# Chunk middles in column groups, the context's keys and values a stage earlier, and softmax sums inverted pair by pair, in a four-layer decoder

## The chip, the cores and the metric

The kernel runs on one core of a Trainium2 chip. The number that counts is the device time of one execution in microseconds (us). Here PE is the matrix engine, PEld its weight loads, DVE the vector engine, ACT the scalar engine, POOL GpSimd and SP the engine that issues most loads.

## The reference, cut to what matters

A decoder of four layers works on 8 batches of 56 tokens with 256 channels, in float32. Each layer is attention, cross attention and a feed-forward part, each added to x and followed by a layer norm. The change bears on three of the twelve stages: layer 1's attention (32 heads of 8, over all keys, quantized in chunks), layer 1's cross attention (16 heads of 16, causal, keys and values from the context, of which the causal mask leaves the first 56 rows) and layer 2's attention (16 query heads of 16, causal).

```python
def _chunk_decompose(x2d):                      # chunks of 32 tokens
    ch_bias = (jnp.max(xp, axis=1, keepdims=True) + jnp.min(xp, axis=1, keepdims=True)) / 2
    xz = xp - ch_bias
    ...
    result = _sym_qdq(xz, scale[:, None, :])
    return (result, ch_bias, T)

def proj(w_orig, w_dq_t, b):
    y = result @ w_dq_t + ch_bias @ w_orig.T
    return y.reshape(-1, H)[:n] + b
...
probs = jax.nn.softmax(attn, axis=-1)
ctx = jnp.einsum('bhqk,bkhd->bqhd', probs, V).reshape(bsz * tgt, H)
r2, cb2, n2 = _chunk_decompose(ctx)
out = (r2 @ WO + cb2 @ o_weight.T).reshape(-1, H)[:n2] + o_bias

x = _layernorm(x + _L1_attn_ref(x, ...))
x = _layernorm(x + _L1_xattn_ref(x, ctx_512, ...))
```

So each projection of layer 1's attention is a product of the quantized remainder, plus a product of the chunk middles (14 chunks of 32 of the 448 tokens) that is the same for the 32 tokens of a chunk, plus a bias.

## The kernel before

Tokens lie in 4 tiles of 112 (two batches each), channels in 2 halves of 128. A scheduler orders each engine's instructions by their dependences; `mm(..., fixed=True)`, `ordered` and `keep_in_program_order` pin those that it must leave where the program has them. Weights of a stage are loaded by SP during the stage before. On-chip sums (PSUM) have eight banks: in these stages two double banks (`bank2`), two single ones (`bank`) and the pair `ps_o`. A float32 product is run by PE in two passes, each its own row of the trace.

**l1_attn** (line 1527). `decompose` (L1485) takes on DVE the maxima and minima of chunks, the middles `mid` (128×28: 14 chunks by 2 channel halves), and the quantized remainder `res`. `middles` (L1556) multiplies `mid` by the undequantized weights: for each of q, k, v in turn two products of 128 rows with 14 weight columns and one of 1 row for the bias, into 14 rows of `ps_gb`; ACT copies these into `gb`, 128 rows of which POOL has zeroed (L1559). Its products are pinned. Then keys and queries `ps_q` (L368, two halves each): two products with `res` and a third with `sel`, a table of 128 rows of which 14 aren't zero and which repeats a chunk's middle over its 32 tokens. `head_values` (L1326) does the same for the values, per batch and per parity of heads, in 64-column groups (`ps_v`, L1340), and copies them into `VX`, zeroed by POOL first (L1332): ACT the even heads, DVE the odd ones. `head_keys` (L1361) spreads keys over heads into `KX`, first half of the batches on DVE, second on POOL (L1370).

`small_heads` (L1379) runs over units (a tile and, with heads of 8, a channel half: 8 units; 4 with heads of 16): scores `ps_s` (PE), their maxima `mx` (DVE L1415), the difference `E` (DVE L1418), the exponential (ACT L1419), sums over keys (DVE L1420), transposes `ps_eT` (PE, ACT copies), and the outputs `ps_o` (PE) of the unit before. After all units one reciprocal of 128×128 sums (L1461), one transpose `ps_rec` (L1463), four DVE products with a block table into `recT` (L1467), then `ps_den`, which spreads the inverted sums over channels, and the product with `num` (L1472).

A second `decompose` of the outputs, `middles` of the output weight and `finish` (L425) follow: per tile `ps_y` (two products with `res2`, one with `sel`), added to X on DVE (L450), moments, then `norm` (L455): DVE L417, ACT's square root (L418), DVE L419 to L422, the normalized X (L459); then PE transposes X to `xT`, ACT copies it (L471).

**l1_xattn** (line 1604). Its k (`ps_k`) is a product of the context (64 rows) and is made after xT is started; KX, VX as above; q (`ps_q`) from `xT`; then `small_heads` and `finish`. **l2_attn** (line 1633) differs in q and k only, and calls the same helpers.

Of the kernel before, what the change touches and what calls it, by code (L numbers as in the profile page):

```python
# [144 lines left out]
def _pack(i):  # L145
# [40 lines left out]
    w["l1a_b"] = np.concatenate([i[p + n + "_bias"] for n in "qkvo"])[None, :]  # L186
    w["l1a_s"] = _beside(_spread(8), (np.arange(T)[None, :] // 32 == np.arange(T // 32)[:, None]).astype(np.float32))

# [76 lines left out]
class Decoder:  # L265
# [1059 lines left out]

    def head_values(self, pool, terms, dk, groups=16):  # L1326

# [5 lines left out]
        for g in range(NB // per):  # L1333
# [10 lines left out]
            for odd in range(2):  # L1344
                rows = slice(odd * 64, odd * 64 + S)
                copy = nc.vector.tensor_copy if odd else nc.scalar.copy
                to, of = VX[rows, g * per : (g + 1) * per], ps[rows, : per * n]
                if dk == 8:
                    to = to.rearrange("p b (x y) n -> p (b x) y n", y=2)
                    of = of.rearrange("p (z y n) -> p z y n", y=2, n=8)  # L1350
                    for y in range(2):
                        at = 16 * y + 8 * odd
                        copy(to[:, :, y, at : at + 8], of[:, :, y, :])
                else:
                    same = 16 // groups
                    to = to.rearrange("p b (x y) n -> p (b x) y n", y=same)[:, :, :, 16 * odd : 16 * odd + 16]
                    of = of.rearrange("p (z n) -> p z n", n=16).unsqueeze(2).to_broadcast([S, per * groups // 2, same, 16])
                    copy(to, of)
        return VX

    def head_keys(self, pool, k, dk):  # L1361

# [3 lines left out]
        for half in range(2):  # L1366
            bs = slice(half * NB // 2, (half + 1) * NB // 2)
            for c in range(2):
                of = k[:, c, :].rearrange("p (b s) -> p b s", s=S)[:, bs].unsqueeze(2).to_broadcast([128, NB // 2, n, S])
                (nc.gpsimd if half else nc.vector).tensor_tensor(KX[:, c, bs], of, hm, ALU.mult)  # L1370
        return KX
# [7 lines left out]
    def small_heads(self, pool, q, KX, VX, dk, causal, scale, spread, oT):  # L1379
# [54 lines left out]
        def outputs(n):  # L1434
            t, unit = units[n]
            eT = ets.pop(n)
            for u in range(2):
                b = 2 * t + u
                for j in range(8):
# [10 lines left out]
                    )  # L1450

        scores(0)
        for n in range(len(units)):
# [3 lines left out]
            if n:  # L1457
                outputs(n - 1)
        outputs(len(units) - 1)
        rec = sums.rearrange("p t i -> p (t i)")  # L1460
        nc.vector.reciprocal(rec, rec)  # L1461
        ps = self.bank("ps_rec")
        nc.tensor.transpose(ps[:, :128], rec, ident)  # L1463
        recT = pool.tile([128, NT, 2, S], F32, bufs=1, name="recT")
        of = ps[:, :128].rearrange("p (u q) -> p u q", u=2)[:, :, :S]
        for t in range(NT):
            nc.vector.tensor_scalar_mul(recT[:, t], of, self.const("blocks")[:, t : t + 1])  # L1467
        nc.scalar.copy(num, acc[:, :, :T])
        for c in range(2):
            ps = self.bank("ps_den")  # L1470
            self.mm(ps[:, :T], [(spread[:, c * 128 : (c + 1) * 128], recT.rearrange("p t u q -> p (t u q)"))])
            nc.vector.tensor_tensor(oT[:, c, :], ps[:, :T], num[:, c, :], ALU.mult)  # L1472
# [54 lines left out]
    def l1_attn(self):  # L1527
# [5 lines left out]
        (bias,) = self.parts("l1a_b")  # L1533
        spread, sel = self.fields("l1a_s", D, T)
        with tc.tile_pool(name="l1a", bufs=2) as pool:
            dT = pool.tile([128, 4, 2, D], F32, bufs=1, name="dT")
# [18 lines left out]

            def middles(mid, first, n):  # L1556

                out = pool.tile([128, n, D], F32, bufs=1, name="gb")
                nc.gpsimd.memset(out, 0.0)  # L1559
                ps = self.bank2("ps_gb")  # L1560
                for j in range(n):
                    self.mm(
                        ps[:G, j // 2, j % 2 * D : (j % 2 + 1) * D],
                        [(mid[:, c * G : (c + 1) * G], wT(first + j, c)) for c in range(2)]
                        + [(self.ones[:1, :G], bias[:, (first + j) * D : (first + j + 1) * D])],
                        fixed=True,
                    )
                for j in range(0, n, 2):
                    m = min(2, n - j)
                    nc.scalar.copy(out[:G, j : j + m, :].rearrange("p j n -> p (j n)"), ps[:G, j // 2, : m * D])  # L1570
                return out

            mid = self.decompose(pool, self.xT, res)
            gb = middles(mid, 0, 3)
            q, k = self.head_queries(pool), pool.tile([128, 2, T], F32, bufs=1, name="k")
            for m in (1, 0):
                ps = self.bank2("ps_q1")
                for o in range(2):
                    at = slice(o * 128, (o + 1) * 128)
                    self.mm(ps[:, o, :T], [(dT[:, m, c, at], res[:, c, :]) for c in range(2)] + [(gb[:, m, at], sel)])  # L1580
                    if m:
# [5 lines left out]
            def value_terms(b, odd):  # L1587
                at = slice(b * S, (b + 1) * S)
                own = lambda a: a.rearrange("p (x y n) -> p x y n", y=2, n=8)[:, :, odd, :]
                return [(res[:, c, at], own(dT[:, 2, c, :])) for c in range(2)] + [(sel[:, at], own(gb[:, 2, :]))]  # L1590

            VX = self.head_values(pool, value_terms, 8, 32)
            oT = pool.tile([128, 2, T], F32, bufs=1, name="oT1")
            self.small_heads(pool, q, KX, VX, 8, False, 8.0**-0.5, spread, oT)
            res2 = pool.tile([128, 2, T], F32, bufs=1, tag="res", name="res2")
            mid = self.decompose(pool, oT, res2)
            gb2 = middles(mid, 3, 1)
            self.finish(
                early=False,
                terms_of=lambda t: [(res2[:, c, self.tok(t)], dT[:, 3, c, :]) for c in range(2)] + [(sel[:, self.tok(t)], gb2[:, 0, :])]  # L1600
            )


    def l1_xattn(self):
        nc, tc, xT = self.nc, self.tc, self.xT
        wq, wo = self.fields("l1x_1", 512, 512)
        wk, wv, cT = self.fields("l1x_2", D, D, T)
        wq, wo = (a.rearrange("p (c n) -> p c n", c=2) for a in (wq, wo))
        (spread,) = self.fields("l1x_t", D)
        with tc.tile_pool(name="l1x", bufs=2) as pool:  # L1610
            q = self.head_queries(pool)
            k = pool.tile([128, 2, T], F32, bufs=1, name="k")
            qps, kps = self.bank2("ps_q"), self.bank2("ps_k")
            for o in range(2):
                self.mm(kps[:, o, :T], [(wk[:DC, o * 128 : (o + 1) * 128], cT[:DC, :])])
            nc.scalar.copy(k, kps[:, :, :T])
            KX = self.head_keys(pool, k, 16)

            def value_terms(b, odd):
                own = wv[:DC, :].rearrange("p (x y n) -> p x y n", y=2, n=16)[:, :, odd, :]  # L1620
                return [(cT[:DC, b * S : (b + 1) * S], own)]

            VX = self.head_values(pool, value_terms, 16)
            for o in range(2):
# [274 lines left out]
```

## Time and profile before

| | us |
|---|---|
| median of 3 runs (lowest to highest) | 1665.28 (1662.88 to 1666.53) |
| profiled execution | 1665.35 |
| its span in the trace | 1663.1 |

The trace's windows give the stages around the change (busy us of each engine, and the granted clock of PE as a share of full speed):

| window | length | PE | DVE | ACT | POOL | clock |
|---|---|---|---|---|---|---|
| 494 to 569: norm, decompose, projections and heads of l1_attn | 75 | 58.64 | 52.19 | 25.37 | 15.54 | 0.82 |
| 569 to 605: second decompose, l1_attn's finish, start of l1_xattn | 36 | 22.40 | 22.38 | 5.12 | 5.26 | 0.67 |
| 605 to 634: heads and finish of l1_xattn | 29 | 21.34 | 20.70 | 11.59 | 3.52 | 0.94 |
| 735 to 782: l2_attn | 47 | 37.71 | 29.74 | 13.74 | 11.56 | 0.96 |

These 187 us are a ninth of the span. The granted clock of the whole execution is 0.926, so the first two windows run at a lower clock than the rest. In the trace's lines a product is written with its weight's shape (rows×columns of weights), the shape of the moving operand, and the number of passes; times are the start in us from the beginning of the span, and the length.

### The profile page before, as it was taken

What the parts mean: (1) busy time and instruction counts of PE and PEld (TensorE: products, weight loads), DVE (VectorE), ACT (ScalarE), POOL (GpSimd) and SP (SyncE); (2) the same over time, 40 slices, a digit from 0 to 9 for tenths busy, and PEclk for the clock granted to TensorE, in tenths of its full rate; (3) what the DMA queues carried; (4) which work ended last, traced back from release to release, by engine and by line L of the source; (5) the groups of instructions that cost most, each with busy time, mean ns of one, the idle gap of its engine ahead of it and who ended that gap; (6) DMA issues with size and microseconds to landing.
All of it is one profiled execution on the core that took longest, in us unless ns stands there. A gap on an engine that the chain in (4) does not pass through costs nothing.

```text
span 1663.1 us, 37875 instructions
## 1 busy us (share of the span) xinstructions
PE 1499.5 (90%) x16428; PEld 894.4 (54%) x16428; DVE 1095.2 (66%) x1793; ACT 625.2 (38%) x915; POOL 323.9 (19%) x302
## 2 busy tenths in 40 slices
PE   7989989999788678998989999899987978999898
PEld 4666435556644344565435555655555834555656
DVE  0575579999475855326569999635474239999633
ACT  2431245655312422103245556332343144566320
POOL 4711511212123010011521122101131000221200
PEclk9999979999897878999988999999997987999989
DMA  9523422323020001222332322121220361323100
GB/s 359 188 79 108 123 56 84 96 83 88 18 87 28 26 27 35 78 70 74 114 86 62 110 78 81 41 64 55 83 64 27 119 172 38 104 72 88 41 1 11
DMA packets 52088, 133.76 MB, mean 80 GB/s; under 512 B 20673, under 2 KB 21137, under 8 KB 51922
## 3 DMA queue, kind: packets, MB, share of 16 engines
q1 hardware_dynamic: 19906, 65.36, 12.0%
q10 hardware_dynamic: 28368, 50.25, 10.8%
q0 software_dynamic: 3648, 15.73, 2.9%
q8 instruction: 129, 2.11, 0.5%
q14 instruction: 37, 0.30, 0.1%
HBM read 119.06 MB, written 6.75 MB: 76 GB/s over the span
## 4 chain that ended last, share of the span: by engine, by line
PE 49%; DVE 9%; issue 8%; ACT 2%; DMA 1%; POOL 1%; ACTq 1%; DVEq 0%; POOLq 0%
PE ps_x L376 17%; PE ps_glu L368 8%; PE ps_y L368 7%; PE ps_qk L1675 2%; DVE sc L376 2%; PE ps_v L1675 2%; PE ps_qh L368 2%; PE ps_big L368 1%; PE ps_y L1675 1%; PE ps_q L368 1%; PE ps_qk L376 1%; PE ps_m L376 1%; PE ps_s L1397 1%; DVE E L1418 1%; DVE mx L1415 1%
## 5 line engine op out<-in xcount | busy, mean ns | idle before, releaser
L376 PE MATMUL ps_x<-kvT,qa 64*128 64x375 f32 x1344 | 310.4, 567 | 29.1 <-DVE sc L376 23.1
L376 ACT ACTIVATE sc<-sc,tops 128x1500 f32<-128x1500 f32 x168 | 259.2, 1544 | 151.7 <-DVE sc L376 118.3
L376 DVE STREAM_TRANSPOSE eT<-sc 128x1536 f32<-128x1536 f32 x168 | 297.1, 1768 | 11.7 <-PE ps_x L376 9.5
L376 PE MATMUL ps_x<-eT,kv 32*64 32x224 f32 x9024 | 257.7, 357 | 3.7 <-issue 3.2
L376 PEld LDWEIGHTS ps_x<-eT,kv 32*64 32x64 f32 x9024 | 197.6, 133 | 70.1 <-issue 59.8
L376 PEld LDWEIGHTS ps_x<-kvT,qa 64*128 64x128 f32 x1344 | 114.3, 201 | 187.2 <-DVE sc L376 160.4
L376 DVE TENSOR_SCALAR_CACHE_REDUCE sc<-ps_x 128x750 f32<-128x750 f32 x168 | 157.3, 936 | 38.4 <-PE ps_x L376 38.2
L376 DVE TENSOR_SCALAR_CACHE_REDUCE sc<-ps_x,tops 128x750 f32<-128x750 f32 x168 | 161.1, 959 | 1.3 <-PE ps_x L376 1.1
L376 POOL TENSOR_TENSOR eT<-eyes,sums 128x224 f32<-128x224 f32 x24 | 13.3, 555 | 453.6 <-DVE sums L376 453.6
L827 POOL TENSOR_TENSOR rope<-rope,turn 96x448 f32<-96x448 f32 x64 | 71.0, 1130 | 65.0 <-DVE turn L825 65.0
L824 DVE TENSOR_TENSOR rope<-ps_big,consts 96x896 f32<-96x896 f32 x32 | 34.8, 1086 | 58.4 <-PE ps_big L368 58.4
L1190 ACT ACTIVATE act<-ps_glu 128x448 f32<-128x448 f32 (+1 forms) x52 | 28.3, 544 | 111.7 <-PE ps_glu L368 108.4
L1194 DVE TENSOR_TENSOR act<-ps_glu,act 128x448 f32<-128x448 f32 x43 | 26.8, 624 | 65.2 <-ACT act L1190 65.1
L418 ACT ACTIVATE rstd<-rstd 112x3 f32<-112x3 f32 (+2 forms) x21 | 4.3, 204 | 166.2 <-DVE rstd L417 166.1
L624 DVE RECIPROCAL rec<-rec 128x896 f32<-128x896 f32 x8 | 46.0, 5753 | 27.0 <-ACT rec L623 27.0
L376 PE MATMUL ps_x<-wm,qa 128*112 128x128 f32 (+1 forms) x336 | 53.5, 318 | 9.7 <-DVE qa L376 9.7
L450 DVE TENSOR_TENSOR X<-X,ps_y 112x256 f32<-112x256 f32 x32 | 13.5, 421 | 70.6 <-PE ps_y L368 70.6
L376 PEld LDWEIGHTS ps_x<-wm,qa 128*112 128x112 f32 x336 | 45.2, 191 | 21.7 <-issue 11.2
L1758 POOL TENSOR_TENSOR qk<-qk,sw 128x896 f32<-128x896 f32 x16 | 33.3, 2083 | 101.3 <-DVE sw L1757 78.8
L376 POOL TENSOR_TENSOR qa<-num,rec 64x448 f32<-64x448 f32 x42 | 47.9, 1140 | 2.9
L754 ACT COPY qa<-ps_qk 64x448 f32<-64x448 f32 x48 | 25.3, 527 | 60.0 <-PE ps_qk L376 46.1
L376 POOL DMA_DIRECT2D kvT<-kvT x24 | 13.7, 573 | 122.7 <-DVE X L450 49.2
(410 smaller groups left out, 2424.2 us busy)
## 6 DMA issues: line engine op xcount, KB each, us to landing
kv<-kv ACTq DMA_DIRECT2D x288, 128.0 KB, 2.7
kvT<-kvT POOLq DMA_DIRECT2D x24, 384.0 KB, 3.5
qa<-qa ACTq DMA_DIRECT2D x24, 224.0 KB, 3.6
raw<-in_ctx ACTq DMA_DIRECT2D x6, 512.0 KB, 4.3
kv<-raw POOLq DMA_DIRECT2D x6, 512.0 KB, 4.2
kvT<-by POOLq DMA_DIRECT2D x6, 512.0 KB, 4.3
l0a_q<-in_l0a_q SPq DMA_DIRECT2D x4, 512.0 KB, 10.6
l0a_c<-in_l0a_c SPq DMA_DIRECT2D x4, 512.0 KB, 8.8
```

What stands on the lines that cost most here:

```text
L368: ins = self.nc.tensor.matmul(out, lhsT, rhs, start=n == 0, stop=n == len(terms) - 1)
L376: call(*args, **kw)
L624: nc.vector.reciprocal(rec, rec)
L754: nc.scalar.copy(flat[rows, :, odd, h // 2 * S : (h // 2 + 1) * S], ps[rows, :T].rearrange("p (b s) -> p b s", b=NB))
L824: nc.vector.tensor_tensor(rope.rearrange("p a (b s) -> p a b s", b=NB), view, cos, ALU.mult)
L827: nc.gpsimd.tensor_tensor(rope[:, half, :], rope[:, half, :], turn[:, 1 - half, :], ALU.add)
L1190: nc.scalar.activation(act, ps[:m, 0, :T], AF.Silu)
L1194: nc.vector.tensor_tensor(act, ps[:m, 1, :T], act, ALU.mult)
L1397: tc.keep_in_program_order(nc.tensor.matmul(*args, **kw))
L1415: nc.vector.tensor_reduce(mx, view, AX.X, ALU.max)
L1675: tc.keep_in_program_order(nc.tensor.matmul(*args, **kw))
L1758: nc.gpsimd.tensor_tensor(qk, qk, sw, ALU.add)
```

## The change

- `middles` takes a list of weights. The contraction half is the outer loop and the weight the inner one; weight j gets rows 32j to 32j+13 of its own bank, so that the three go to three column groups of PE. `gb` has one column block, with weight j in rows 32j to 32j+13, copied by ACT in one copy a weight; it is no longer zeroed. The table `sel` is repeated each 32 rows, and the third term of `ps_q`, `ps_v` and `ps_y` uses 14 rows of it instead of 128.
- `small_heads` inverts the 128×32 sums of a tile as soon as its units are done, in the loop. Four transposes of 128×32 replace the one of 128×128; they put all tiles into 32 rows, so that one copy of 32×448 replaces the four products with the block table, and `ps_den` contracts 32 rows. All three stages use it.
- `l1x_context` makes l1_xattn's k and VX inside l1_attn, between `small_heads` and the second `decompose`, in a pool of its own opened ahead of l1_attn's. Both halves of the values are copied by ACT.
- `head_keys` with `alone` runs all four KX products on DVE, in program order; l1_xattn uses it.

In issue order, on PE `ps_k` and l1_xattn's `ps_v` move from behind l1_attn's finish to between `ps_den` and the second `ps_top`; on POOL that stage's VX memset moves ahead of l1_attn's KX, and its two KX products are gone. SP's loads are the same in the same order.

```diff
     w["l1a_b"] = np.concatenate([i[p + n + "_bias"] for n in "qkvo"])[None, :]
-    w["l1a_s"] = _beside(_spread(8), (np.arange(T)[None, :] // 32 == np.arange(T // 32)[:, None]).astype(np.float32))
+    w["l1a_s"] = _beside(_spread(8), (np.arange(T)[None, :] // 32 == np.arange(128)[:, None] % 32).astype(np.float32))
...
-    def head_values(self, pool, terms, dk, groups=16):
+    def head_values(self, pool, terms, dk, groups=16, copies=None):
...
                 rows = slice(odd * 64, odd * 64 + S)
-                copy = nc.vector.tensor_copy if odd else nc.scalar.copy
+                copy = (copies or (nc.scalar.copy, nc.vector.tensor_copy))[odd]
                 to, of = VX[rows, g * per : (g + 1) * per], ps[rows, : per * n]
...
-    def head_keys(self, pool, k, dk):
+    def head_keys(self, pool, k, dk, alone=False):
...
                 of = k[:, c, :].rearrange("p (b s) -> p b s", s=S)[:, bs].unsqueeze(2).to_broadcast([128, NB // 2, n, S])
-                (nc.gpsimd if half else nc.vector).tensor_tensor(KX[:, c, bs], of, hm, ALU.mult)
+                to = KX[:, c, bs]
+                if alone:
+                    self.ordered(nc.vector.tensor_tensor, to, of, hm, ALU.mult)
+                else:
+                    (nc.gpsimd if half else nc.vector).tensor_tensor(to, of, hm, ALU.mult)
         return KX
...
+        per = len(units) // NT
         scores(0)
...
                 outputs(n - 1)
+            if n % per == per - 1:
+                nc.vector.reciprocal(sums[:, n // per], sums[:, n // per])
         outputs(len(units) - 1)
-        rec = sums.rearrange("p t i -> p (t i)")
-        nc.vector.reciprocal(rec, rec)
         ps = self.bank("ps_rec")
-        nc.tensor.transpose(ps[:, :128], rec, ident)
-        recT = pool.tile([128, NT, 2, S], F32, bufs=1, name="recT")
-        of = ps[:, :128].rearrange("p (u q) -> p u q", u=2)[:, :, :S]
         for t in range(NT):
-            nc.vector.tensor_scalar_mul(recT[:, t], of, self.const("blocks")[:, t : t + 1])
+            tc.keep_in_program_order(nc.tensor.transpose(ps[:32, t * 128 : (t + 1) * 128], sums[:, t], ident))
+        recT = pool.tile([32, NT * 2, S], F32, bufs=1, name="recT")
+        nc.vector.tensor_copy(recT, ps[:32].rearrange("p (u q) -> p u q", q=64)[:, :, :S])
         nc.scalar.copy(num, acc[:, :, :T])
...
             ps = self.bank("ps_den")
-            self.mm(ps[:, :T], [(spread[:, c * 128 : (c + 1) * 128], recT.rearrange("p t u q -> p (t u q)"))])
+            self.mm(ps[:, :T], [(spread[:32, c * 128 : (c + 1) * 128], recT.rearrange("p u q -> p (u q)"))])
             nc.vector.tensor_tensor(oT[:, c, :], ps[:, :T], num[:, c, :], ALU.mult)
...
+        self.l1x = ExitStack()
+        self.l1x_pool = self.l1x.enter_context(tc.tile_pool(name="l1x", bufs=1))
         with tc.tile_pool(name="l1a", bufs=2) as pool:
...
-            def middles(mid, first, n):
-                out = pool.tile([128, n, D], F32, bufs=1, name="gb")
-                nc.gpsimd.memset(out, 0.0)
+            def middles(mid, ms):
+                out = pool.tile([128, D], F32, bufs=1, name="gb")
                 ps = self.bank2("ps_gb")
-                for j in range(n):
-                    self.mm(
-                        ps[:G, j // 2, j % 2 * D : (j % 2 + 1) * D],
-                        [(mid[:, c * G : (c + 1) * G], wT(first + j, c)) for c in range(2)]
-                        + [(self.ones[:1, :G], bias[:, (first + j) * D : (first + j + 1) * D])],
-                        fixed=True,
-                    )
-                for j in range(0, n, 2):
-                    m = min(2, n - j)
-                    nc.scalar.copy(out[:G, j : j + m, :].rearrange("p j n -> p (j n)"), ps[:G, j // 2, : m * D])
-                return out
+                banks = [ps[:, 0], ps[:, 1], self.bank("ps_gb1") if len(ms) > 2 else None]
+                for k in range(3):
+                    for j, m in enumerate(ms):
+                        of = bias[:, m * D : (m + 1) * D]
+                        lhsT, rhs = (self.ones[:1, :G], of) if k == 2 else (mid[:, k * G : (k + 1) * G], wT(m, k))
+                        self.ordered(nc.tensor.matmul, banks[j][32 * j : 32 * j + G, :D], lhsT, rhs, start=k == 0, stop=k == 2)
+                for j in range(len(ms)):
+                    nc.scalar.copy(out[32 * j : 32 * j + G], banks[j][32 * j : 32 * j + G, :D])
+                return lambda j: (out[32 * j : 32 * j + G], sel[32 * j : 32 * j + G])
             mid = self.decompose(pool, self.xT, res)
-            gb = middles(mid, 0, 3)
+            gb = middles(mid, (1, 0, 2))
             q, k = self.head_queries(pool), pool.tile([128, 2, T], F32, bufs=1, name="k")
...
                     at = slice(o * 128, (o + 1) * 128)
-                    self.mm(ps[:, o, :T], [(dT[:, m, c, at], res[:, c, :]) for c in range(2)] + [(gb[:, m, at], sel)])
+                    mine, sel_ = gb(1 - m)
+                    self.mm(ps[:, o, :T], [(dT[:, m, c, at], res[:, c, :]) for c in range(2)] + [(mine[:, at], sel_)])
                     if m:
...
                 own = lambda a: a.rearrange("p (x y n) -> p x y n", y=2, n=8)[:, :, odd, :]
-                return [(res[:, c, at], own(dT[:, 2, c, :])) for c in range(2)] + [(sel[:, at], own(gb[:, 2, :]))]
+                mine, sel_ = gb(2)
+                return [(res[:, c, at], own(dT[:, 2, c, :])) for c in range(2)] + [(sel_[:, at], own(mine))]
...
             self.small_heads(pool, q, KX, VX, 8, False, 8.0**-0.5, spread, oT)
+            self.l1x_context()
             res2 = pool.tile([128, 2, T], F32, bufs=1, tag="res", name="res2")
             mid = self.decompose(pool, oT, res2)
-            gb2 = middles(mid, 3, 1)
+            mine, sel_ = middles(mid, (3,))(0)
             self.finish(
                 early=False,
-                terms_of=lambda t: [(res2[:, c, self.tok(t)], dT[:, 3, c, :]) for c in range(2)] + [(sel[:, self.tok(t)], gb2[:, 0, :])]
+                terms_of=lambda t: [(res2[:, c, self.tok(t)], dT[:, 3, c, :]) for c in range(2)] + [(sel_[:, self.tok(t)], mine)]
             )
...
+    def l1x_context(self):
+        pool = self.l1x_pool
+        wk, wv, cT = self.fields("l1x_2", D, D, T)
+        k = pool.tile([128, 2, T], F32, name="k")
+        ps = self.bank2("ps_k")
+        for o in range(2):
+            self.mm(ps[:, o, :T], [(wk[:DC, o * 128 : (o + 1) * 128], cT[:DC, :])], fixed=True)
+        self.nc.scalar.copy(k, ps[:, :, :T])
+        def value_terms(b, odd):
+            own = wv[:DC, :].rearrange("p (x y n) -> p x y n", y=2, n=16)[:, :, odd, :]
+            return [(cT[:DC, b * S : (b + 1) * S], own)]
+        self.l1x_made = k, self.head_values(pool, value_terms, 16, copies=(self.nc.scalar.copy,) * 2)
...
         wq, wo = self.fields("l1x_1", 512, 512)
-        wk, wv, cT = self.fields("l1x_2", D, D, T)
         wq, wo = (a.rearrange("p (c n) -> p c n", c=2) for a in (wq, wo))
         (spread,) = self.fields("l1x_t", D)
-        with tc.tile_pool(name="l1x", bufs=2) as pool:
+        with self.l1x, tc.tile_pool(name="l1q", bufs=2) as pool:
+            k, VX = self.l1x_made
             q = self.head_queries(pool)
-            k = pool.tile([128, 2, T], F32, bufs=1, name="k")
-            qps, kps = self.bank2("ps_q"), self.bank2("ps_k")
-            for o in range(2):
-                self.mm(kps[:, o, :T], [(wk[:DC, o * 128 : (o + 1) * 128], cT[:DC, :])])
-            nc.scalar.copy(k, kps[:, :, :T])
-            KX = self.head_keys(pool, k, 16)
-            def value_terms(b, odd):
-                own = wv[:DC, :].rearrange("p (x y n) -> p x y n", y=2, n=16)[:, :, odd, :]
-                return [(cT[:DC, b * S : (b + 1) * S], own)]
-            VX = self.head_values(pool, value_terms, 16)
+            KX = self.head_keys(pool, k, 16, alone=True)
+            qps = self.bank2("ps_q")
             for o in range(2):
```

## The prediction

> **What bounds the kernel.** The page first. PE is busy for nine tenths of the span, and the row of granted clock falls below 9 at the stage borders; a change beside PE pays only where PE waits.
>
> ```profile
> span 1663.1 us, 37875 instructions
> PE 1499.5 (90%) x16428; PEld 894.4 (54%) x16428; DVE 1095.2 (66%) x1793; ACT 625.2 (38%) x915; POOL 323.9 (19%) x302
> ```
>
> Then the chain of waits over l1_attn, l1_xattn and l2_attn, which hold all of the edits (columns: start, length, work that carried the chain):
>
> ```profile
> 508.94 8.32 PE ps_gb L368 x18
> 517.26 9.69 PE ps_q L368 x18
> ...
> 530.20 4.94 PE ps_v L1340 x86
> 535.14 1.66 PE ps_s L1397 x16
> ...
> 581.66 8.35 PE ps_y L368 x24
> ...
> 597.82 3.35 PE ps_k L368 x4
> 601.17 3.30 PE ps_q L368 x4
> ```
>
> From 508.9 to 535.1 PE never rests: middles (ps_gb), keys and queries (ps_q), values (ps_v). ps_y is l1_attn's output, ps_k the context's keys. Then the PE windows of 3.41 us on whose borders the granted clock changes here (columns: window, length, PE busy and instructions, clock):
>
> ```profile
> 38.03:41.44 3.41, 3.41 (x32) 1.00 0.44 168
> 41.44:44.85 3.41, 3.41 (x25) 0.50 0.00 0
> ...
> 509.06:512.47 3.41, 3.41 (x8) 0.50 0.00 0
> 512.47:515.89 3.42, 3.42 (x9) 0.50 0.35 101
> ...
> 519.30:522.71 3.41, 3.41 (x6) 0.50 0.00 0
> 522.71:526.13 3.42, 3.42 (x11) 1.00 0.00 0
> ```
>
> PE is wholly busy from 509.06, but at half clock until 522.71. And the full window at 38.03, spent on products that use 8 weight rows, is followed by half clock. Windows full of 128-row products lift the clock; windows full of thin ones don't.
>
> **The change, part by part** (minus is faster; profiled execution 1665.35 us, span 1663.1; the median shown, 1665.28, is the same within 0.1).
>
> A. First norm, ahead of decompose. The chain has DVE's normalization (L459) from 498.85 for 2.26, though its tiles elsewhere take 0.35 each (1.38 for four at 594.60). It comes loose when POOL's VX memset ends (497.44 + 3.51 = 500.95). Ahead of that memset POOL clears gb (496.62, 0.74), which goes; memset and norm end about as much earlier: **−0.7**.
>
> B. Middles. Before: three weights in turn, each 4 passes (1.82) and 2 bias passes (0.96), 8.32 in all. After: k outer, three column groups. PE then waits for `res`, which DVE had done at 515.33; ps_q started at 517.19, when ps_gb let go of PE. At most 517.19 − 515.33 = 1.86 can be had, as long as the new ps_gb takes under 6.4. One third of 8.32 is 2.8, two thirds 5.5: both fit. **−1.8** (0 if the groups don't run beside each other). The missing memset and the 3 copies of 14×256 instead of 2 lie beside ps_q.
>
> C. `sel` terms of 14 rows instead of 128 (ps_q, ps_v, ps_y). Stream length is the same, 448, 128 or 256 columns; but each such term now has another tile shape (32 rows) than the two before it. Such a change is in the trace already, in l3_attn, with 16-row terms between 128-row ones:
>
> ```profile
> 1144.17 1.67 PE L1675 MATMUL ps_qk<-hT,l3a_k 128*128 128x448 f32 x4
> 1145.77 1.13 PE L368 MATMUL ps_low<-l3a_l 16*128 16x512 f32 x4
> 1146.82 1.77 PE L1675 MATMUL ps_qk<-hT,l3a_q 128*128 128x448 f32 x4
> ```
>
> From start to start, plain passes of 448 and 512 columns take 0.376 and 0.427 here, but 0.469 the last one before the change of shape and 0.532 the first one after it: 0.09 + 0.10, so **0.2 a border**, both ways alike. The second part is a weight load that no longer runs under the pass before it. With 64 weight columns (l0_attn's ps_q to ps_v: 0.469 for 0.376, then 0.147 for 0.109; its ps_d likewise) it is 0.14. At half clock the bias excursions of ps_gb cost 0.21 for two borders with 14 weight columns; the first ps_y pass with 128 took 0.560 for 0.427, and with a load of 0.17 laid open a border is 0.3. The Trainium skill (TensorEngine Tiling (Array Packing), Key Properties) speaks against the change in the same sense: a change of tiling mode drains TensorE. It gives no price; the row's is used.
> By the issue order of the changed kernel the stretch from ps_q to ps_v has 21 such borders, 6 among 128-column weights and 15 among the values' 64-column ones: 6 × 0.2 + 15 × 0.14 = **+3.3**.
> The clock makes this larger. A ps_q group is 4 full passes and 2 of 32 rows: 4 × 0.747 = 3.0 of full array in 6 × 0.747 + 0.5 = 5.0 us, some 60%. Windows at half clock in this trace went up only when 80% or more of the time was full-array work (580.74:584.16 with 2.50 busy stayed). So the lift at 522.71 comes in most positions of the window grid one window later, which costs 3.41 / 2 = 1.7; I take 0.8 of it, **+1.3**. C's head: 3.3 + 1.3 = **+4.6** (bounds: 0, if borders are hidden by loads ahead; +16, if the values too stay at half clock).
>
> D. Loop of small_heads in l1_attn: 4 reciprocals of 128×32 (0.36 by 128×28's 0.33) instead of one of 128×128 at the end (0.95). DVE has 0.26 to 0.34 idle before each score, so they fit: 0 to +0.1, taken 0.
>
> E. ps_y of l1_attn, 8.35 before: half clock to 587.57, then full.
>
> ```profile
> 580.74:584.16 3.42, 2.50 (x6) 0.50 0.30 107
> 584.16:587.57 3.41, 3.41 (x9) 0.50 0.01 2
> 587.57:590.98 3.41, 2.90 (x19) 1.00 0.00 0
> ```
>
> The window at 584.16, full of 128-row passes, lifted it. After, a tile is 4 passes of 0.427 = 1.71, a border, 2 thin passes 0.85, a border: 3.1 with 1.71 of full array, 55%; never 80%. Four tiles: 4 × 2.56 + 7 × 0.3 = 12.3, so **+4.0**. Here the rule and the rows part. The skill (TensorE: Matmul & The Clock Gate, Part 1) lets the clock follow PE's busy-ness over a window of about 3.4 us; by it the full window lifts the clock as before, and only 7 borders × 0.2 = +1.5 is paid (and +3.3 in the head). But by it 509.06:512.47 should also have lifted the clock, and it didn't. The row decides.
>
> F. Second norm, l1_attn's finish. Gone from DVE's chain: two VX copies, and the wait of L417 (0.91 against 0.17 elsewhere), whose end 592.08 is the end of POOL's VX memset (590.25 + 1.81):
>
> ```profile
> 591.17 0.91 DVE L417 TENSOR_SCALAR rstd<-mv 112x4 f32<-112x4 f32 x1
> ...
> 592.96 0.69 DVE L1358 COPY VX<-ps_v 56x512 f32<-56x512 f32 x1
> ...
> 593.88 0.69 DVE L1358 COPY VX<-ps_v 56x512 f32<-56x512 f32 x1
> ```
>
> 0.74 + two times 0.7 = **−2.2**. The memset now stands in front of l1_attn's KX on POOL, long before the norm.
>
> G. Context's keys and values a stage ahead. ps_k leaves the path after xT (3.3). Its new place, with ps_v 2.0, is PE's idle 569.3 to 574.2 under DVE's decompose: 3.5 of 4.9 used, ACT's five copies (0.9 + 4 × 0.55) end about 0.8 before ps_tmax needs a bank: 0, or up to +1 if they are late. But ps_k also warmed the array: the second ps_q pair ran in 1.77. Without it the pair and the scores run at half clock in about two thirds of grid positions, 1.5 to 2.4 lost. Taken: 0.3 × 3.3 + 0.7 × 0.9 = **−1.6**. KX, now 4 × 1.0 on DVE after the norm (ordered), ends some 4 us before q: nothing.
>
> H. Reciprocals and tails of the 16-wide heads. In l2_attn DVE runs two sums, then mx of the third unit with no gap (760.17 + 2.19, 762.27); two reciprocals of 0.36 stand in between, one more before E: **+0.9**. In l1_xattn 0.9 of idle covers the two: **+0.2**. The old one (0.95) lay under ps_o's last outputs and gave nothing. In the three tails one copy of 448 columns (0.6) replaces four products (1.06), and 3 more transposes cost 0.3: 3 × −0.2 = **−0.6**.
>
> Sum: −0.7 − 1.8 + 4.6 + 0 + 4.0 − 2.2 − 1.6 + 0.9 + 0.2 − 0.6 = +2.8: **1668.2** from 1665.35.
>
> **Rivals.**
> 1 (the other side): the clock follows busy time, not array use. C's head is +3.3, E +1.5: 2.8 − 1.3 − 2.5 = −1.0, 1664.3; if borders are besides hidden by loads ahead, 4.8 less again, 1659.5. It decides below a border price of about 0.1. For it: ps_gb's 1-row excursion costs only 0.21. Against: windows 38.03 and 509.06.
> 2. Values stay at half clock: l1_attn's ps_v is 16 × 3 terms, a third thin, with a border at nearly every third; if its first window doesn't lift the clock none does: +16 instead of +4.6, 1680. For: 60% of use. Against: the scheduler groups thin terms of neighbouring values, which leaves the later windows fuller; 2 in 10 of grid positions.
> 3. Column groups share one moving path and run in turn: B is 0 (8.3 is over 6.4), 1670.0. For: no row shows three groups of such passes at once. Against: ps_o's 64 passes of 56 columns, in four column groups, took 1.26, 0.020 each, where 56 of 448 columns alone would be 0.047.
> 4. The moved context is late (ACT holds ps_tmax's bank, or the transfers of its operands, loaded in the same order as before): +1 to +2, 1669.7.
>
> **Numbers.** Forecast 0.50, own range 1665 to 1672; rival 1 0.19; rival 2 0.12; rival 3 0.11; rival 4 0.08. A difference of 0.2%, 3.3 us, is what can be told from none: bounds 1662.0 and 1668.6. Faster: two thirds of rival 1, and a little of the forecast's spread, 0.15. Slower: rivals 2 and 3, most of 4, and under half of the forecast, 0.50; same 0.35. The range 1661 to 1675 leaves out rival 2 and rival 1's lowest end.
>
> **What would show it.** ps_gb in under 4 us and ps_q's start at `res`'s end (B). Starts of ps_q and ps_v passes 0.1 to 0.3 wider at thin terms; ps_q's start to ps_s's at about 22.5 instead of 17.9 (C). ps_y near 12 us with clock 0.50 throughout (E); if its third window shows 1.00, rival 1 holds. L417 at 0.17 and no copy between L421 and L422 (F). mx right after xT's chain with no ps_k, l1_xattn's ps_q at 0.50 (G). Reciprocal rows of 0.36 in front of mx in l2_attn (H). A wait of ps_tmax, on ACT's VX copies, would prove rival 4. The forecast is wrong if neither ps_y nor ps_q grows.

## The result, and the profile after

The changed kernel takes 1670.66 us (median of 20 executions, 1660.21 to 1682.72); the kernel before takes 1661.63 (median of 20, 1652.88 to 1666.53). The medians lie 9.0 us apart. The ratio, the figure used from here on, is **1.0067, 95% interval 1.0051 to 1.0083**, about 11 us. Two things stand beside the number. The execution that the prediction took as its base, 1665.35, was one of the slower ones of the kernel before. And the new kernel spreads over 22 us where the old one spread over 14.

The profiled execution of the changed kernel is also one of its slower ones, 1676.4. Its page (span; busy time, share and instructions of each engine):

```profile
span 1674.4 us, 37887 instructions
PE 1509.5 (90%) x16437; PEld 896.1 (54%) x16437; DVE 1089.8 (65%) x1793; ACT 626.9 (37%) x918; POOL 317.7 (19%) x298
```

PE has 9 instructions more and is busy 10 us longer: the passes take longer. The chain of waits of the changed kernel says where (start, length, work):

```profile
508.71 1.10 DVE res L1486
511.16 1.10 DVE res L1489
512.39 11.84 PE ps_q L369 x18
525.16 2.64 PE ps_q L369 x6
527.81 6.92 PE ps_v L1341 x86
534.73 1.66 PE ps_s L1403 x16
...
567.74 3.35 PE ps_den L369 x4
571.09 3.28 PE ps_k L369 x4
574.37 3.62 PE ps_v L1341 x32
582.37 1.10 DVE res L1486
584.82 1.10 DVE res L1489
585.97 12.48 PE ps_y L369 x24
601.33 1.77 PE ps_xT L471 x8
604.08 3.37 PE ps_q L369 x4
608.13 3.35 PE ps_q L369 x4
```

ps_gb is no longer in the chain: what ps_q waits for is `res`. From ps_q to the scores 22.3 us pass (17.9 before). ps_y takes 12.48 (8.35). After the heads come ps_den at 3.35 (1.75 before), and ps_k and ps_v, which were to be hidden. In l1_xattn both ps_q pairs run at half clock (3.35; the second took 1.77 before).

Between the copies of xT that close the stages, this gives, in us of the two profiled executions:

| from xT to xT | before | after |
|---|---|---|
| l1_attn, up to l1_xattn's input | 94.17 | 103.51 |
| l1_xattn | 41.54 | 41.02 |
| l1's feed-forward | 97.57 | 98.64 |
| l2_attn | 47.66 | 50.02 |

### The profile page after: what moved, and what is told of

It is laid out like the page before. It is cut to its first block, busy times and chain, and to the rows that moved or that the text cites. A ratio compares the mean times of both kernels' runs of the same rounds, so it can differ in the third digit from the quotient of the medians.

```text
span 1674.4 us, 37887 instructions
## 1 busy us (share of the span) xinstructions
PE 1509.5 (90%) x16437; PEld 896.1 (54%) x16437; DVE 1089.8 (65%) x1793; ACT 626.9 (37%) x918; POOL 317.7 (19%) x298
## 3 DMA queue, kind: packets, MB, share of 16 engines
q1 hardware_dynamic: 19906, 65.36, 11.9%
## 4 chain that ended last, share of the span: by engine, by line
PE 49%; DVE 9%; issue 8%; ACT 2%; ACTq 1%; POOL 1%; DMA 0%; DVEq 0%; POOLq 0%
PE ps_x L377 16%; PE ps_glu L369 8%; PE ps_y L369 8%; PE ps_qk L1690 2%; DVE sc L377 2%; PE ps_v L1690 2%; PE ps_qh L369 2%; PE ps_big L369 1%; PE ps_q L369 1%; PE ps_y L1690 1%; PE ps_qk L377 1%; PE ps_v L1341 1%; ACTq L377 1%; PE ps_m L377 1%; DVE E L1424 1%
## 5 line engine op out<-in xcount | busy, mean ns | idle before, releaser
L377 PEld LDWEIGHTS ps_x<-wm,qa 128*112 128x112 f32 x336 | 45.7, 193 | 22.2 <-issue 11.1
## 6 DMA issues: line engine op xcount, KB each, us to landing
l0a_q<-in_l0a_q SPq DMA_DIRECT2D x4, 512.0 KB, 10.7
```

What stands on the lines that cost most here:

```text
L377: call(*args, **kw)
```

## The experiments

Each kernel is compared with the kernel before by ratio and 95% interval. One per mille is 1.66 us. "From ps_x to ps_y" is from first pass to first pass. In these traces the clock changes only at borders that lie whole multiples of 3.41 us apart (called the grid of windows here); the windows below are cut there.

### Full rows in the third terms

```diff
-                out = pool.tile([128, D], F32, bufs=1, name="gb")
+                out = pool.tile([128, len(ms), D], F32, bufs=1, name="gb")
+                nc.gpsimd.memset(out, 0.0)
...
-                return lambda j: (out[32 * j : 32 * j + G], sel[32 * j : 32 * j + G])
+                return lambda j: (out[:, j, :], sel)
```

> The changed kernel with third terms of 128 rows again (gb zeroed, each weight in its own column block at rows 32j, sel unsliced); column groups stay. Theory (thin terms drain PE at each border and keep the clock down): ps_q's start to ps_s's start falls from 22.3 to about 17.9, ps_y from 12.5 to about 8.4 with a window at 1.00, and some 0.7 for the memset comes back: 8 us faster than the changed kernel, about 1.001 of the kernel before. Rival (only the borders cost, the clock is a matter of the grid): 4.8 less and 0.7 more, about 1.004.

Measured: 1.0011 (0.9995 to 1.0028). Of the 11 us, 9 come back, although the zeroing of gb comes back too and costs some 0.7 (term A below). ps_q's start to ps_s's is 17.17, and ps_y takes 7.36. Its chain:

```profile
510.35 9.05 PE ps_q L369 x18
522.65 4.94 PE ps_v L1341 x86
575.16 7.36 PE ps_y L369 x24
```

Windows of PE in this kernel, during ps_y (window, length, PE busy and instructions, clock, DMA share, GB/s):

```profile
575.64:579.05 3.41, 3.41 (x9) 0.50 0.03 11
579.05:582.47 3.42, 3.42 (x16) 1.00 0.03 7
```

After one window full of 128-row passes the clock is 1.00. In the changed kernel, over the same passes with thin third terms:

```profile
585.21:588.62 3.41, 2.65 (x6) 0.50 0.18 71
588.62:592.03 3.41, 3.41 (x8) 0.50 0.03 7
592.03:595.45 3.42, 3.42 (x8) 0.50 0.00 0
595.45:598.86 3.41, 2.98 (x6) 0.50 0.00 0
```

Two whole windows without a gap that the profile sees, and the clock stays at 0.50.

### The same in ps_y alone

```diff
+                if len(ms) == 1:
+                    nc.gpsimd.memset(out, 0.0)
...
+                if len(ms) == 1:
+                    return lambda j: (out, sel)
```

> The changed kernel with 128-row third terms in ps_y alone; ps_q and ps_v keep the 14-row ones. Splits the 9 us that full rows gave back. If ps_y's part is the deterministic 4.4 that its traces show and the head's is about as much on average (17.9 becoming 22.3, or 34.0 in some executions), this is 4 us faster than the changed kernel: 1.004 of before, and its times keep the wide spread of the changed kernel. Rival: the head costs nothing on average; then 1.002 or less.

Measured: 1.0037 (1.0021 to 1.0053). So ps_y is worth 3.0 per mille, 5.0 us, and the projections and values another 2.6 per mille, 4.3 us, each with an uncertainty of about 4 us. The traces agree in size: ps_y takes 12.48 in the changed kernel, 8.43 in this one and 7.36 in full_rows (the last two differ by where their passes lie on the grid), and ps_q's start to ps_s's is 22.26, 22.25 and 17.17.

### Do rows keep the clock down, or the borders between shapes?

At a border passes start up to 0.1 us later than within a run of one shape (part C of the prediction) while the busy time shows no gap, so the two windows above could be less full than they look. Here every pass of ps_y has 14 rows, and no border is left between them:

```diff
-                terms_of=lambda t: [(res2[:, c, self.tok(t)], dT[:, 3, c, :]) for c in range(2)] + ...
+                terms_of=lambda t: [(res2[:G, c, self.tok(t)], dT[:G, 3, c, :]) for c in range(2)] + ...
```

> The changed kernel with only 14 of 128 channel rows of res2 in ps_y's first two terms; 228 of 256 channels of the output projection are left out. All 24 passes then have one shape, with no borders between them and PE busy all the time. If the clock follows how much of the array is used, ps_y stays at half clock: 24 passes of 0.427, about 10.2, and windows of 3.41 busy at 0.50. If borders (drained time) kept the clock down in the changed kernel, it rises after the first full window: 7.5 to 8.5.

This kernel was run once, for its trace. Its PE windows during ps_y:

```profile
586.14:589.55 3.41, 2.64 (x6) 0.50 0.14 55
589.55:592.97 3.42, 3.42 (x9) 0.50 0.02 7
592.97:596.38 3.41, 3.41 (x9) 0.50 0.00 0
```

24 passes at 0.427 from start to start (the first 0.558), 586.91 to 597.49, and the clock doesn't rise. With 128 rows it rose after the first full window. So PE's busy time alone doesn't lift the clock; it depends on how many rows of the array the passes use.

### small_heads as before

```diff
-            if n % per == per - 1:
-                nc.vector.reciprocal(sums[:, n // per], sums[:, n // per])
+        rec = sums.rearrange("p t i -> p (t i)")
+        nc.vector.reciprocal(rec, rec)
...
-            tc.keep_in_program_order(nc.tensor.transpose(ps[:32, t * 128 : (t + 1) * 128], sums[:, t], ident))
+        nc.tensor.transpose(ps[:, :128], rec, ident)
...
-            self.mm(ps[:, :T], [(spread[:32, c * 128 : (c + 1) * 128], recT...)])
+            self.mm(ps[:, :T], [(spread[:, c * 128 : (c + 1) * 128], recT...)])
```

> The changed kernel with small_heads as before (one reciprocal of 128x128, one transpose, four products with the block table, ps_den over 128 rows). Theory A (products of 32 rows let the clock fall at the end of the heads, ps_den 1.75 to 3.35 in two or three stages, and l2_attn's reciprocals stand in the chain): 4 to 6 us faster than the changed kernel, about 1.004 of before. Rival B (the half clock of ps_den in the one profile is the grid's position; the prediction's terms hold): 0.5 faster, about 1.0065 of before.

Measured: 1.0029 (1.0011 to 1.0047), 6.3 us faster than the changed kernel, with an uncertainty of 4. That is far more than the prediction's half microsecond. The profiled execution of this kernel happens to show the prediction's second rival. Its chain:

```profile
510.93 15.26 PE ps_q L369 x18
526.19 1.64 PE ps_v L1341 x10
527.83 5.07 PE ps_q L369 x6
532.90 12.13 PE ps_v L1341 x86
```

The values took 12.13 instead of 6.92 and PE stayed at 0.50 from 498 to 556: ps_q's start to ps_s's is 34.03. So 2 of the 6 profiled executions with thin terms in the head ended so (this one and the one of `context_back`), 3 at 22.2, and one at 20.0. This can add to the spread of 22 us, but isn't shown to be its cause: den_full_end below has full rows in the head and spreads over 20 (1645.27 to 1664.90).

What decides can be read off the six traces. First the passes of ps_q here, then the one run of full passes in the changed kernel:

```profile
514.19 1.86 PE L369 MATMUL ps_q<-l1a_s,gb 14*128 14x448 f32 x2
515.97 4.85 PE L369 MATMUL ps_q<-res,dT 128*128 128x448 f32 x6
520.75 1.86 PE L369 MATMUL ps_q<-l1a_s,gb 14*128 14x448 f32 x2
```

```profile
517.44 3.95 PE L369 MATMUL ps_q<-res,dT 128*128 128x448 f32 x6
```

The changed kernel's window 516.94 to 520.36 holds two thin passes for its first 0.5 us and full ones after. Weighted by rows (128 or 14, each pass counted to the next one's start), it uses 87% of the rows, and the clock rises at its end. In old_tail a border at 518.54 cuts the six full passes in two, and no window until the scores uses more than 78%, though each from 511.71 on is wholly busy. In the four executions that rose early the window before the rise used 83 to 96%.

### ps_den over 128 rows

```diff
+        recT = pool.tile([128, NT * 2, S], F32, bufs=1, name="recT")
+        nc.gpsimd.memset(recT, 0.0)
...
-            self.mm(ps[:, :T], [(spread[:32, c * 128 : (c + 1) * 128], recT...)])
+            self.mm(ps[:, :T], [(spread[:, c * 128 : (c + 1) * 128], recT...)])
```

> The changed kernel with recT of 128 rows, of which 96 are zeroed once by POOL, so that ps_den contracts 128 rows; reciprocals by pairs and the four transposes stay. Theory A with rows as the cause: ps_den at 1.75 in most stages, 2 to 4 us faster than the changed kernel. If the clock has already fallen before ps_den (idle PE in the last unit), ps_den stays at 3.35 and the time stays within 1 us of the changed kernel.

Measured: 1.0074 (1.0047 to 1.0100). No gain, but with eight executions and a wide interval: against the changed kernel it is 0.7 per mille slower, with an uncertainty of 3. In the trace, from xT to xT, l1_attn took 101.00 (103.50 in the changed kernel) and l1_xattn 38.73 (41.02; from ps_y's first pass to the next xT 10.98 for 11.87), but in l2_attn ps_den ran at half clock again (50.32 for 50.02). Taken alone, the time speaks against the rows of ps_den; two later kernels speak for them.

### The context's keys and values where they were

The edit puts l1_xattn back as it was before the change, without `l1x_context` and with KX half on POOL.

> The changed kernel with l1_xattn's k and VX made in l1_xattn again, KX half on POOL. By the prediction's terms F and G the move was worth 3.8 (2.2 in the norm, 1.6 for ps_k), so undoing it costs 3.8: 1.009 of before. Rival (the moved products run at half clock, hold ps_top for 1.9 and ps_tmax's bank for 0.6, and leave q at half clock): the move was worth about 1, undoing it changes the time by less than 1.5 us.

Measured: 1.0100 (1.0067 to 1.0132), 5.5 us slower than the changed kernel, with an uncertainty of 6. That agrees with the 3.8 that the prediction gave the move, but doesn't tell it from zero; the pair groups_only and rows_tail below does. What the move costs shows in the changed kernel's trace. DVE's rows there:

```profile
575.75 0.17 DVE L1510 TENSOR_TENSOR t<-cmax 128x14 f32<-128x14 f32 x1
578.31 0.28 DVE L1514 TENSOR_REDUCE top<-ps_top 14x1 f32<-14x128 f32 x1 [2.38 <-PE ps_top L1512]
579.55 0.19 DVE L1518 COPY tmax<-ps_tmax 128x28 f32<-128x28 f32 x1 [0.96 <-PE ps_tmax L1516]
```

`t` was done at 575.9, and ps_top followed 1.9 later than before the change, behind ps_v; ps_tmax followed 0.6 later, behind ACT's VX copy. Both are hidden where these products run at full clock (rows_tail's trace has 6.73 from ps_den to ps_top, as before the change), but here ps_den, ps_k and ps_v ran at 0.50.

### Full rows and the old small_heads together; column groups alone

> Full rows and small_heads as before: of the change only the column groups and the moved context are left. By deterministic parts (reciprocals 1.05 in l2_attn and 0.85 in l1_xattn) 1.5 to 2 us faster than full rows alone: 0.9997 of before. If the 6 us that the old tail gave the changed kernel were its own and not the grid's, 0.9975.

Measured: **0.9974 (0.9955 to 0.9993)**, faster than both kernels. The old small_heads is again worth 3.7 per mille (uncertain by 2.5), so it wasn't the grid's luck.

> Of the change only the middles in column groups, with full rows. Prediction's term B: ps_q starts at res's end, 1.7 us earlier than before: 0.999 of before. The moved context's worth is rows_tail against this: by terms F and G 3.8 for it less the 2.5 of ps_top's and ps_tmax's waits, so rows_tail is 1 us faster; if it is slower, the move loses by itself.

Measured: 1.0003 (0.9987 to 1.0019). Against it rows_tail, which adds the moved context, is 2.9 per mille faster, 4.8 us with an uncertainty of 4; in the traces its l1_attn is 3.2 shorter from xT to xT and its l1_xattn 1.4. The column groups do what they say: in the changed kernel's trace the 18 passes take about 2.9 instead of 8.3, and PE then waits 3.74 for `res`:

```profile
505.79 1.90 PE L377 MATMUL ps_gb<-l1a_w,mid 128*14 128x256 f32 x12
507.61 1.04 PE L377 MATMUL ps_gb<-l1a_b,consts 1*14 1x256 f32 x6
512.39 1.09 PE L369 MATMUL ps_q<-res,dT 128*128 128x448 f32 x1 [3.74 <-DVE res L1489]
```

12 passes in 1.82 is the time of 4 alone. xT to ps_q fell from 13.59 to 11.88 in this kernel's trace too; the whole time doesn't show these 1.7 us, which its interval of ±2.7 us can hold.

Steps from the changed kernel back to the one before thus are, in per mille: thin rows 5.6, small_heads 3.7, the moved context −2.9, column groups 0.3; together the measured 6.7. Each of the first three is the difference of two ratios and uncertain by some 2.3 to 2.5 per mille, the last by 1.6.

### The context split

Both start from `rows_tail`. In the first, k's product follows ps_gb, and the values use the double banks of the scores; in the second only k is moved.

```diff
             gb = middles(mid, (1, 0, 2))
+            self.l1x_keys()
...
-            self.l1x_context()
+            self.l1x_values()
```

> As rows_tail, with l1_xattn's k product in PE's wait for res (3.7 us after the column groups) and its values in banks of the score pair, so that neither holds ps_top or ps_tmax: den to top 6.7 and top to y 7.4 as before the change, 1 to 3 us faster than rows_tail, 0.9985 of before. Rival: k runs over res's end or VX's copies hold num, and it is no faster than rows_tail.

> rows_tail with l1_xattn's k product in PE's wait for res, the values where rows_tail has them. If the moved context still costs where the clock is low at the end of the heads (den to top over 6.7), 0.5 to 1.5 us faster than rows_tail, 0.997 of before; if it is hidden there in most executions, the same as rows_tail.

Measured: 0.9983 (0.9965 to 1.0002) and 0.9973 (0.9957 to 0.9990). Neither is faster than rows_tail. In the first the scheduler drew the values into the last units of the heads: in its chain ACT's four VX copies (0.58 each) stand around the last exponential and ahead of the last eT copies, and ps_s to ps_den grew from 31.68 to 33.97. That is the expectation's rival, at other copies than it named. In the second nothing was gained: in rows_tail's trace den to top is 6.73 and top to y 7.37, so the moved context was hidden there already. (The second kernel's own trace has 34.13 and 8.31, because the clock fell twice: at the start of the heads and ahead of ps_den.)

### What in small_heads costs 6 us

One reciprocal after the loop again, all else of the new small_heads kept, with full rows in the third terms:

> full_rows with one reciprocal of 128x128 after the loop again; the four transposes of 128x32, the one copy and the 32-row ps_den stay. The old small_heads was worth 6 us in two pairs of kernels, the prediction had it at 0.5. Theory A (the cause is the reciprocals in DVE's chain of the loop, directly 1.05 in l2_attn and 0.8 in l1_xattn, and by the longer loop a clock that falls before ps_den and ps_y): most of it comes back, 0.998 of before, ps_den of l2_attn at 1.78. Theory B (the cause is the tail: thinner transposes and ps_den): it stays at 1.001 of before.

Measured: 1.0000 (0.9979 to 1.0021). The interval holds both theories, so the time doesn't decide. In the trace the loop of l2_attn is shorter (19.77 from ps_s to ps_den, 20.50 in full_rows), but ps_den to ps_y there is still 3.28, which speaks against the reciprocals as the main cause. The last kernel adds 128 rows in ps_den to it:

> recip_end with ps_den over 128 rows (recT zeroed once by POOL below its 32 rows): of the new small_heads only the four transposes of 128x32 and the one copy are left. In the traces so far every kernel with a 32-row ps_den has l1_xattn's ps_y partly at half clock (ps_y's first pass to the next xT 11.9 to 12.3) and every one with 128 rows has not (10.7 to 11.0). If that is the tail's cost, this reads 10.7 to 11.0 there and 1.78 from l2_attn's ps_den to its ps_y, and the time is that of rows_tail, 0.9975 of before. If the transposes are the cost, l2_attn's ps_den stays at 3.2 and the time at 1.000.

Measured: **0.9968 (0.9953 to 0.9982)**, not to be told from rows_tail, and 3.2 per mille, 5.3 us, faster than recip_end for 96 rows of zeros, with an uncertainty of 4. The windows of PE around l1_xattn's ps_den, first with 32 rows (recip_end), then with 128 (den_full_end):

```profile
623.67:627.08 3.41, 2.69 (x32) 1.00 0.02 5
627.08:630.49 3.41, 3.39 (x8) 0.50 0.02 0
630.49:633.90 3.41, 1.98 (x9) 1.00 0.14 36
```

```profile
619.78:623.20 3.42, 2.61 (x10) 1.00 0.02 5
623.20:626.61 3.41, 3.41 (x15) 1.00 0.02 0
```

The first window of each holds the end of the heads and ps_den, with 2.69 and 2.61 of busy time; after the one with 32 rows the clock falls, and ps_y, in the window behind it, pays:

```profile
625.30 1.76 PE L369 MATMUL ps_den<-recT,l1x_t 32*128 32x448 f32 x4 [0.71 <-DVE recT L1473]
627.10 5.37 PE L369 MATMUL ps_y<-l1x,oT 128*112 128x256 f32 x16
```

```profile
620.92 1.77 PE L369 MATMUL ps_den<-recT,l1x_t 128*128 128x448 f32 x4 [0.77 <-DVE recT L1475]
622.73 3.96 PE L369 MATMUL ps_y<-l1x,oT 128*112 128x256 f32 x16
```

ps_den itself takes the same time. This is so in every profiled kernel: from l1_xattn's first ps_y pass to the end of the next xT copy, 11.9 to 12.3 in the six with 32 rows, 10.7 to 11.0 in the eight with 128.

In l1_attn the same rows lift a clock that had fallen. In both traces it fell 3.0 or 3.1 us before ps_den began, and ps_den took 3.35. With 32 rows (recip_end) it stayed down through ps_k and ps_v, which follow; with 128 (den_full_end) it rose 3.7 us after ps_den's start, and ps_den to ps_y took 15.71 instead of 18.22. First recip_end, then den_full_end:

```profile
568.47 3.35 PE L369 MATMUL ps_k<-l1x 64*128 64x448 f32 x4
571.75 3.66 PE L1341 MATMUL ps_v<-l1x 64*56 64x128 f32 x32
```

```profile
568.12 1.98 PE L369 MATMUL ps_k<-l1x 64*128 64x448 f32 x4
570.03 1.96 PE L1341 MATMUL ps_v<-l1x 64*56 64x128 f32 x32
```

## Why the prediction was right or wrong

Right in the direction and, by its range, in the time: forecast 1668.2, measured 1670.66. That the time lay in the range was in part luck. The difference to before was forecast as 2.8 and is 11 by the ratio; the base lay 3.7 above the median of 20 executions, and from that median the same sum gives 1664.4, below its own range. By the four steps of the experiments, forecast and measured: thin rows with the zeroing of gb (A, C, E) 7.9 and 9.3; small_heads (D, H) 0.5 and 6.1; moved context (F, G) −3.8 and −4.8; column groups (B) −1.8 and 0.5. One step of the four was mis-sized beyond its uncertainty of 3 to 4 us.

- **A, first norm, −0.7.** Right in the traces: the normalization took 2.26 before and 1.58 after, ending with the memset of VX. From the end of ps_y's last pass to the end of xT's copy it is 7.0 to 7.1 in all eight traced kernels that zero gb's 128×768, and 6.0 to 6.4 in the six that don't. Its share of the whole time wasn't tested alone.
- **B, column groups, −1.8.** Right in the trace: xT to ps_q 13.59, then 11.88. Rival 3 is refuted. In the whole time not told from zero.
- **C, thin terms in the head, +4.6.** Right: 17.87 to 22.26 in the trace, 4.3 in the times. The border was priced at 0.14 among the values; 12 passes took 0.94 for 0.66, with two borders, 0.14 each. (The trace has 23 borders where 21 were counted.) The 80% at which the prediction let the clock rise lies between the 78% and 83% of the six traces. Rival 2 wasn't a rival of the forecast but a share of its executions.
- **D, reciprocals in l1_attn's loop, 0.** Not told apart: from ps_s to ps_den 33.1 us against 32.5, but these hold a changed clock too.
- **E, ps_y, +4.0.** Right: 8.35 to 12.48, at 0.50 throughout. Rival 1, the clock by busy time, is refuted by the kernel without borders, and with it the reading of the Trainium skill (TensorE: Matmul & The Clock Gate, Part 1) as a rule of busy time.
- **F and G, norm and moved context, −3.8.** Right in sum: −4.8 between groups_only and rows_tail, −5.5 between context_back and the changed kernel (uncertain by 4 and 6). L417 (L418 in the changed kernel) is at 0.18 and no copy stands between the two lines that L421 and L422 became. Of rival 4, 2.5 was paid in the profiled execution, as a price of the half clock that came before it.
- **H, the tails, +0.5: this step failed.** The prediction counted reciprocals (0.9 in l2_attn; its trace has 1.07 from ps_s to ps_den) and copies, and passed over that ps_den now contracts 32 rows, though it had just worked out in C and E what thin rows do to the clock. It priced the instruction that became thin at nothing, since its own time stays the same. What is paid stands in the windows behind it. In the changed kernel's trace ps_y takes 5.3 in l1_xattn and 5.4 in l2_attn, each for 3.96 before, and the feed-forward part, where the clock rises later, 98.64 for 97.57; in l1_attn ps_k and ps_v stay at half clock, 2.5 in the pair above. Measured in the times: 6 us for the whole of small_heads in two pairs of kernels, 5.3 for the rows of ps_den alone in one pair, and nothing for them in den_full.

Open is what else small_heads costs, and why den_full gained nothing in its time while den_full_end did. In l2_attn ps_den itself ran at half clock (3.35 for 1.74). Its own rows can't be the cause: the clock had fallen before it began, 3.0 to 3.9 us before in seven of the eight kernels with the new small_heads (in two of them it was back in time for ps_den), and in none of the six with the old. den_full_end is the eighth. Its loop is 1.3 us shorter than den_full's (18.96 from ps_s to ps_den for 20.27), and its ps_den began 1.57 us after a border of the grid, den_full's 3.18. That would fit a loop made longer by the reciprocals, but recip_end, with its one reciprocal behind the loop, lost the clock too. One execution of each was traced; more were not tried.

## What to carry to other kernels

Before a product is cut to fewer rows or columns, ask what the clock makes of it: padding with zeros cost no time in the pass itself here (ps_den 1.76 with 32 rows, 1.77 with 128), and it kept the clock up for the passes after it. Price such an edit in the window behind it, not at the instruction. Packing small products into column groups can pay where PE is what ends last; here it shortened ps_gb by 5.4 us, and the path by only 1.7, up to the wait that stands next, `res`.

## What the runs showed of the hardware that was not expected

- Zeros count as use. In full_rows a third of ps_y's passes have 128 rows of which 114 are zero in one operand, and the clock rises after one window (ps_y 7.36; 12.48 with 14 rows). 10 us of wholly busy passes of 14 rows don't lift it.
- In the head of l1_attn a wholly busy window that used 78% of the array's rows (old_tail, weighted as there) left the clock at 0.50, and one of 83% (den_full) lifted it.
- A single pair of products (ps_den in l1_xattn, 1.77 us) decided over the clock of the next 3.41 us, the same way in all 14 traces.
- A clock once up is held by work that doesn't lift it. The values with thin thirds ran at 1.00 where the clock had risen before them (the changed kernel, 520.36) and at 0.50 to their end where it hadn't (old_tail, until 556.09), in the same order of instructions: 12 us in one stage, decided by how the passes lie on the grid of windows.
